# Attention scores of a two-layer macaron block in two float32r parts: maxima and weights on the two halves of TensorE's array

## The chip, the cores and the metric

The kernel runs on one core of a Trainium2 chip. The metric is the device time of one execution in microseconds. Before the change the median of three runs is 1638.24 us (1638.05 to 1641.87). Engines are written as the profile writes them: PE is TensorE's matmuls, PEld its weight loads, DVE VectorE, ACT ScalarE, POOL GpSimd, SP the engine whose queue issues most DMAs.

## What is computed

The input x has 16 batches of 512 tokens of width 128, in float32. Six sublayers follow each other, each on a layer norm of x and added to x:

```
x = x + 0.5 * kan(norm(x))        # per-feature two-layer perceptron on 64 features
x = x + attention(norm(x))        # 16 heads of width 8, 4 key heads, rotary, causal softmax
x = x + 0.5 * kan(norm(x))
x = x + 0.5 * experts(norm(x))    # 8 experts, each takes its 128 best tokens of a batch
x = x + recurrence(norm(x))       # gated linear recurrence over the tokens
x = x + 0.5 * experts(norm(x))
```

The change is in the attention:

```
q, k, v = x @ Wq, x @ Wk, x @ Wv              # 16, 4 and 4 heads of width 8; rotary on q and k
att = einsum('bhqd,bhkd->bhqk', q, k) / sqrt(8)
att = softmax(where(causal, att, lowest))
y = einsum('bhqk,bhkd->bhqd', att, v) @ Wo
```

The choice of the experts' tokens depends on everything before it, so the scores are computed to nearly float32 precision, out of products of low-precision parts.

## The kernel before

Every engine's order of instructions is written out by hand: generators emit work, and a loop calls them in turns. There are 44 turns per batch (`TURNS = NR * len(BANKS)`, 4 packs of 11 banks). In a turn the loop steps `weights(b)` and `maxima(b+1)` by one bank each, and then every generator in the lists `urgent` and `sides` by one step; what a step emits into `later` comes out at the start of the next turn. Side work asks `need` and `bank` for room: a turn has budgets of 1.5 us for PE, 1.15 for DVE, 0.85 for ACT and 1.45 for POOL, and a generator that finds too little waits for the next turn. An engine carries out its instructions in exactly the order in which the turns emitted them.

A batch goes through these steps:

- `kan` (first sublayer): norm, transposes (L319), two products of 512 columns (L339), eight activations (L372) with products into strips of 32 columns of the array, two groups of four (L366), and the output product (L387).
- `attn_in`: norm, products for queries (L425), rotated queries (L431), keys (L437, 512 columns on 64 columns of the array) and values (L445). VectorE multiplies by the rotary table (L426, L432, L438, L446), POOL adds. `parts` splits queries [128, 512] and keys [32, 512] into three bf16 parts: one copy on ACT (L397) and three steps on POOL (L400, L403, L406) each. `spread` writes the parts to DRAM, and DMAs on SP read them back into **packs**: `kp` with one batch's keys (3 buffers) and `qp` with four query heads of one key head r (10 buffers). A pack's 72 rows are the nine products of three parts by three parts, 8 dimensions each.
- `maxima(b+1)`: for each of four packs r and each of eleven banks, score products of queries by keys over the 72 rows into a PSUM bank `ps_sc` (L612, bf16, query tokens on the output's rows). A bank is one head of 512 or 384 keys, two heads of 256, or four of 128; banks of several heads first get a causal mask by a product with an identity (L608). VectorE then takes the row maxima (L617, L622). Two banks alternate.
- `max_rows`: for each half (two packs) VectorE negates the maxima and splits them into three bf16 parts (L632 to L638), TensorE transposes them (L643), and DMAs bring them by way of DRAM into rows 96 to 98 of the query packs. The key packs hold ones there, so that a product over 99 rows is a score less its row's maximum.
- `weights(b)`: the same scores transposed, keys on the output's rows, over 99 rows into `ps_st` (L675), then the exponential on ACT into `pt` (L678) and the causal cut on POOL (L680). In the last batch every other bank is called `ps_sl`.
- `outputs(b, r)`: `pt` by the values, four heads into four strips of 32 columns, 512, 384, 256 and 128 tokens wide (L698, PSUM `ps_av`, one buffer), a copy on ACT (L703), four transposes (L711), and a division on VectorE (L715, L716).
- `stage_out`: output product (L731), the next `kan`, norm and router scores (L751).

So `maxima` of a batch runs beside `weights` of the batch ahead of it. In one turn TensorE has all matmuls of a bank of weights, then all of a bank of maxima, then side work. After the last batch the packs' memory is taken by the experts' weights and tokens: weights are loaded at the start of the last batch, into packs that it doesn't use. The experts' phase (`experts`, L967, L980, with its combine in float32r, L931) takes the rest of the time.

Of the kernel before, what the change touches and what calls it, by code (L numbers as in the profile page):

```python
# [8 lines left out]
F32 = mybir.dt.float32  # L9
# [8 lines left out]
P = 128  # L18
S = 512
# [10 lines left out]
NQP = 10  # L30
NKP = 3
MXR = 96
# [16 lines left out]
def tile_macaron(  # L49
# [51 lines left out]
    with ExitStack() as ph:  # L101
# [54 lines left out]
        nc.scalar.dma_start(out=gate_sb, in_=gate_in)  # L156
        rbias = cst.tile([P, 2, NV], F32, name="rbias")

        w2d = cst.tile([P, 2, NV, MH], F32, name="w2d")
        eye4 = cst.tile([P, MH], F32, name="eye4")  # L160
# [6 lines left out]
        KR = NR * HD  # L167
        wq = cst.tile([D, NH, HD], F32, name="wq")
        nc.sync.dma_start(out=wq, in_=wq_in.rearrange("k (h d) -> k h d", d=HD))
        wk = cst.tile([D, 2, NR, HD], F32, name="wk")  # L170
        nc.sync.dma_start(out=wk[:, 0, :, :], in_=wk_in.rearrange("k (h d) -> k h d", d=HD))
# [3 lines left out]
        nc.sync.dma_start(out=wo, in_=wo_in)  # L175
# [3 lines left out]
        for b in range(1, B):  # L179
            load(b)  # L180
        hh = HD // 2
        wqr = cst.tile([D, NH, HD], F32, name="wqr")
        identb = cst.tile([P, P], BF16, name="identb")
# [3 lines left out]

        QP = [qkp.tile([P, NG, S], BF16, name=f"qp{i}", tag=f"qp{i}") for i in range(NQP)]
        KP = [qkp.tile([P, NR, S], BF16, name=f"kp{i}", tag=f"kp{i}") for i in range(NKP)]
        ROWS = slice(0, MXR + 3)  # L190

        def packed(b):
            return [QP[(NR * b + r) % NQP] for r in range(NR)], KP[b % NKP]

# [199 lines left out]
        def parts(r, dst, copies, **work):  # L394

            yield from need(**work)
            copies(dst[:, 0, :], r)  # L397
            yield
            yield from need(pool=1.15)
            nc.gpsimd.tensor_tensor(dst[:, 1, :], r, dst[:, 0, :], ALU.subtract)  # L400
            yield
            yield from need(pool=1.15)
            nc.gpsimd.tensor_tensor(r, r, dst[:, 0, :], ALU.subtract)  # L403
            yield
            yield from need(pool=1.3)
            nc.gpsimd.tensor_tensor(dst[:, 2, :], r, dst[:, 1, :], ALU.subtract)  # L406
            yield

        def spread(part, heads, name):

            scr = tc.dram_tile([3, HD, heads, S], BF16, name=name)
            for i in range(3):
                nc.sync.dma_start(out=scr[i].rearrange("d h t -> h d t"), in_=part[:, i, :])
            return scr

        def attn_in(b, st):
            _, xT = yield from norm(x[b])
            ka = w1p.tile([KR, S], F32, name="rope_ka")
            kb = w1p.tile([KR, S], F32, name="rope_kb")
            ta = w1p.tile([P, S], F32, name="rope_a")  # L420
            tb = w1p.tile([P, S], F32, name="rope_b")
            qpart = w1p.tile([P, 3, S], BF16, name="qpart")
            kpart = w1p.tile([KR, 3, S], BF16, name="kpart")
# [12 lines left out]
            pk = yield from bank([2 * KR, S], F32, "ps_pk", 0.9)  # L436
            nc.tensor.matmul(pk, lhsT=wk.rearrange("k w h d -> k (w h d)"), rhs=xT, start=True, stop=True)  # L437
            later.append(lambda: nc.vector.tensor_mul(ka, pk[0:KR, :], rope[0:KR, 0, :]))  # L438
# [3 lines left out]
            take(dve=0.7)  # L442
            pv = yield from bank([P, NT, KR], F32, "ps_v", 0.9)
            for c in range(NT):
                nc.tensor.matmul(pv[:, c, :], lhsT=xT[:, bass.ts(c, P)], rhs=wv, start=True, stop=True)  # L445
            later.append(lambda: nc.vector.tensor_mul(kb, pk[KR : 2 * KR, :], rope[KR : 2 * KR, 1, :]))  # L446
            yield
            take(dve=0.7)
            freed()
            qp_steps = parts(ta, qpart, nc.scalar.copy, act=0.6)  # L450
# [3 lines left out]
            nc.gpsimd.memset(va[:, :, :, HD:32], 0.0)  # L454
            nc.gpsimd.memset(va[:, :, :, HD : HD + 1], 1.0)
            later.append(lambda: nc.vector.tensor_copy(va[:, :, :, 0:HD], pv.rearrange("p c (r d) -> p c r d", d=HD)))
            yield
            take(dve=0.3)
# [3 lines left out]
            def keys():  # L462
                yield from need(pool=1.25)
                nc.gpsimd.tensor_tensor(ka, ka, kb, ALU.add)
                yield
                yield
                yield
                yield from parts(ka, kpart, nc.scalar.copy, act=0.6)

            yield from together(qp_steps, keys())  # L470
            qp, kp = packed(b)

            ks = spread(kpart, NR, f"ks{b}")
            qs = spread(qpart, NH, f"qs{b}")
            N = 3 * HD
            for j in range(3):
                nc.sync.dma_start(
                    out=kp[j * N : (j + 1) * N, :, :],
                    in_=ks[j].rearrange("d r t -> d (r t)").unsqueeze(0).to_broadcast([3, HD, NR * S]),
                )  # L480
            for r in range(NR):
                while taken[0] < NR * b + r - NQP + 1:
                    yield
                src = qs[:, :, r * NG : (r + 1) * NG, :].rearrange("i d h t -> (i d) (h t)")
                nc.sync.dma_start(out=qp[r][0 : 3 * N, :, :],
                                  in_=src.unsqueeze(0).to_broadcast([3, N, NG * S]))
            yield

        def centered(ps, w):

            ps = ps[:, 0 : w.shape[1]]
            nc.tensor.matmul(ps, lhsT=center, rhs=w, start=True, stop=True)
            nc.vector.tensor_copy(w, ps)
# [6 lines left out]
        def cleared(pack):  # L500

            nc.vector.memset(pack[MXR - 32 : MXR, :, :], 0.0)

        def keys_cleared(i):

            cleared(KP[i])
            nc.vector.memset(KP[i][MXR : MXR + 3, :, :], 1.0)

        def prepare():
# [26 lines left out]
            centered(psc[:, 1, :], wk[:, 0, :, :].rearrange("k h d -> k (h d)"))  # L536
# [5 lines left out]
            nc.vector.tensor_copy(wk[:, 1, :, 0:hh], wk[:, 0, :, hh:HD])  # L542
            nc.vector.tensor_copy(wk[:, 1, :, hh:HD], wk[:, 0, :, 0:hh])
# [5 lines left out]
            make_identity(nc, identb)  # L549
            nc.gpsimd.memset(causal[:, 0 : S - P], 0.0)  # L550
            make_causal_mask(nc, own, NEG)
            for i in range(1, NR):
                cleared(QP[i])
                yield
            for _ in range(16):
                yield
            for i in range(NR, NQP):
                if i - NR < NKP - 1:
                    keys_cleared(i - NR + 1)
                yield  # L560
                yield
                cleared(QP[i])
                yield
                yield
# [33 lines left out]
        def maxima(b, st):  # L598
            qp, kp = packed(b)
            for half in range(2):  # L600
                maxs = w2p.tile([P, NT, NH // 2], F32, name="maxs")
                for r in (2 * half, 2 * half + 1):
                    for c, gs in BANKS:
                        n = (c + 1) * P
                        v = in_bank(scp.tile([P, S], F32, name="ps_sc"), gs)
                        alone = len(gs) == 1
                        if not alone:
                            nc.tensor.matmul(v[:, :, n - P : n], lhsT=identb,  # L608
                                             rhs=own.unsqueeze(1).to_broadcast([P, len(gs), P]),
                                             start=True, stop=False, skip_group_check=True)  # L610
# [642 lines left out]
```

## Time and profile before

| | |
|---|---|
| median of three runs | 1638.24 us |
| the profiled execution's own time | 1638.15 us |
| its span on the engines | 1636.4 us |
| mean clock that TensorE was granted | 0.979 of full |
| PE, DVE, ACT, POOL busy | 1527.1, 1173.9, 988.6, 977.5 us |
| up to the first exponential | 119.1 us |
| the 15 batches that have maxima beside weights | 119.1 to 910.2 us |
| last batch | 910.2 to about 960 us |
| experts, recurrence, experts | about 960 to 1636.4 us |

How to read it: the span is from the first to the last instruction on the engines; the own time has what lies around it too. A group's line gives source line, engine, operation, written and read tile, shapes, count, then busy time and mean length of one instruction in ns. An fp32 matmul has two records (two passes), a bf16 or float32r matmul one. `72*128` stands for rows and columns of the array that a matmul uses: 128*32 is a strip of 32 columns, 64*128 half of the rows. A matmul's record includes the way through the array, so that records overlap; the distance from start to start is what the engine spends.

### The profile page before, as it was taken

The page shows a single profiled execution, that of the slowest core. Times are in us where ns is not written, and L with a number is a line of the kernel's source. Part 1 is how long each engine was busy: PE and PEld are TensorE (multiplying, and loading weights), DVE is VectorE, ACT ScalarE, POOL GpSimd, SP SyncE. Part 2 cuts the span into 40 slices and gives each one's busy share as a digit, 9 for nine tenths or more (in the row PEclk, how much of TensorE's full clock was granted, in tenths as well). Part 3 has the DMA queues.
Part 4 walks back from the last instruction along what each step waited for, and adds up shares of the span by engine and source line. Part 5 has one row for each costly group of instructions (what it writes and reads, how often), then busy time and mean ns, then how long its engine had stood idle before and what let it go on. Part 6 is the DMA issues. An engine that isn't in the chain of part 4 may idle for free.

```text
span 1636.4 us, 33218 instructions
## 1 busy us (share of the span) xinstructions
PE 1527.1 (93%) x11881; PEld 1062.5 (65%) x11881; DVE 1173.9 (72%) x3646; ACT 988.6 (60%) x1884; POOL 977.5 (60%) x1455
## 2 busy tenths in 40 slices
PE   5689999999999999999998899999998999999998
PEld 2234444454445444445444479999997999999998
DVE  6578878888888888888898345975579755873343
ACT  3336677877778777777766865444443444444443
POOL 2634566566655664665564666667665566756673
PEclk9779999999999999999999999999999999999999
DMA  5110110111011100110122113223322223323332
GB/s 128 64 69 24 55 54 26 42 55 53 32 40 52 57 25 36 57 47 29 42 71 69 51 44 69 59 54 72 72 68 56 66 62 72 78 51 74 67 67 58
DMA packets 99290, 92.74 MB, mean 57 GB/s; under 512 B 13245, under 2 KB 87686, under 8 KB 98886
## 3 DMA queue, kind: packets, MB, share of 16 engines
q1 hardware_dynamic: 76732, 67.72, 13.4%
q0 software_dynamic: 21584, 22.89, 7.7%
q8 instruction: 93, 1.52, 0.4%
q14 instruction: 71, 0.58, 0.1%
q10 hardware_dynamic: 810, 0.02, 0.0%
HBM read 59.07 MB, written 35.45 MB: 58 GB/s over the span
## 4 chain that ended last, share of the span: by engine, by line
PE 70%; DVE 20%; ACT 4%; issue 3%; POOL 2%; DMA 1%; SPq 0%; DVEq 0%; POOLq 0%; ACTq 0%
PE ps_h L967 12%; PE ps_y L980 12%; PE ps_av L698 7%; PE ps_st L675 6%; PE ps_sc L612 6%; DVE below L617 5%; PE acc L931 4%; PE ps_kg L366 3%; PE ps_s L339 3%; PE ps_t L319 3%; DVE ln_st L288 2%; ACT pt L678 2%; PE ps_ko L387 2%; DVE wk L801 2%; DVE tok L799 1%
## 5 line engine op out<-in xcount | busy, mean ns | idle before, releaser
L680 POOL TENSOR_SCALAR_AFFINE_SELECT pt<-pt 128x128 f32<-128x128 f32 (+2 forms) x704 | 253.2, 367 | 326.3 <-ACT pt L678 321.2
L678 ACT ACTIVATE pt<-ps_st 128x512 f32<-128x512 f32 x682 | 368.0, 563 | 94.5 <-PE ps_st L675 89.0
L617 DVE CUSTOM_DVE_ANT_0 below<-ps_sc,causal 128x512 bf16<-128x512 f32 (+1 forms) x512 | 315.2, 616 | 79.8 <-PE ps_sc L612 64.5
L870 POOL DMA_INDIRECT xg<-xnd,tokI x256 | 254.4, 994 | 86.7 <-issue 38.3
L969 ACT ACTIVATE mo<-ps_h 128x512 f32<-128x512 f32 x256 | 152.8, 597 | 228.1 <-PE ps_h L967 227.2
L967 PE MATMUL ps_h<-xin,mw 128*128 128x128 f32 x2048 | 273.8, 277 | 0.0
L980 PE MATMUL ps_y<-mw,mo 128*128 128x128 f32 x2048 | 272.0, 276 | 0.0
L612 PE MATMUL ps_sc<-kp,qp 72*128 72x512 bf16 (+3 forms) x1024 | 258.9, 304 | 12.6 <-DVE maxs L617 7.6
L675 PE MATMUL ps_st<-qp,kp 99*128 99x512 bf16 x992 | 249.9, 303 | 16.7 <-ACT pt L678 16.2
L967 PEld LDWEIGHTS ps_h<-xin,mw 128*128 128x128 f32 x2048 | 251.8, 193 | 12.8 <-issue 10.8
L980 PEld LDWEIGHTS ps_y<-mw,mo 128*128 128x128 f32 x2048 | 250.8, 193 | 0.1
L675 PEld LDWEIGHTS <-kp 99*128 99x128 bf16 x1024 | 94.4, 100 | 175.9 <-issue 158.4
L372 ACT ACTIVATE kan_h<-kan_s,rbias,kw 128x512 f32<-128x512 f32 x256 | 205.6, 812 | 4.1 <-PE ps_kg L366 4.1
L997 POOL DMA_INDIRECT sum<-mo,tokI x93 | 151.4, 1628 | 75.7 <-ACT mo L969 16.6
L698 PE MATMUL ps_av<-pt,va 128*32 128x512 f32 (+3 forms) x2048 | 165.2, 440 | 0.0
L622 DVE TENSOR_REDUCE maxs<-ps_sc 128x2 f32<-128x512 f32 (+1 forms) x192 | 130.1, 685 | 35.0 <-PE ps_sc L612 34.5
L612 PEld LDWEIGHTS <-qp 72*128 72x128 bf16 x1024 | 96.0, 99 | 80.4 <-issue 58.0
L698 PEld LDWEIGHTS ps_av<-pt,va 128*32 128x32 f32 x2048 | 53.5, 109 | 93.6 <-issue 42.5
L295 POOL TENSOR_TENSOR ln_rstd<-ln_rstd,mhalf 128x4 f32<-128x4 f32 x96 | 102.7, 1069 | 8.0
L294 POOL TENSOR_SCALAR ln_rstd<-ln_mv 128x4 f32<-128x4 f32 x96 | 22.0, 229 | 119.6 <-DVE ln_mv L292 119.4
L319 PE MATMUL ps_t<-ident,kan_x 128*128 128x128 f32 x384 | 63.5, 289 | 30.8 <-DVE kan_x L309 21.4
L986 DVE SCALAR_TENSOR_TENSOR ye<-ps_y,gainT,ye 128x128 fp32r<-128x128 f32 x83 | 28.8, 347 | 83.4 <-ACT ye L983 83.1
(196 smaller groups left out, 2487.5 us busy)
## 6 DMA issues: line engine op xcount, KB each, us to landing
qp<-qs SPq DMA_DIRECT2D x64, 288.0 KB
xnd<-kan_x SPq DMA_DIRECT2D x32, 256.0 KB
sum<-x SPq DMA_DIRECT2D x62, 128.0 KB
qs<-qpart SPq DMA_DIRECT2D x48, 128.0 KB
kp<-ks SPq DMA_DIRECT2D x48, 96.0 KB
x<-in_L_attn_x_dram SPq DMA_DIRECT2D x16, 256.0 KB
mw<-in_L_ffn_w_dram SPq DMA_DIRECT2D x16, 256.0 KB
xg<-xnd,tokI POOLq DMA_INDIRECT x256, 2.6
```

The lines of the kernel that those rows point to most:

```text
L372: nc.scalar.activation(h, sk[half], AF.Relu, bias=rbias[:, half, v : v + 1], scale=kw1[:, half, v : v + 1])
L612: nc.tensor.matmul(v[:, u, 0:n], lhsT=qp[r][0 : 9 * HD, g, bass.ts(c, P)], rhs=kp[0 : 9 * HD, r, 0:n], start=alone, stop=(u == len(gs) - 1 ...
L617: nc.vector.tensor_tensor_reduce(below[:, 0:n], v[:, 0, 0:n], causal[:, S - n : S], 1.0, LOWEST, ALU.add, ALU.max, accum_out=maxs[:, c, h ...
L675: nc.tensor.matmul(v[:, u, 0:n], lhsT=kp[ROWS, r, bass.ts(c, P)], rhs=qp[r][ROWS, g, c * P : S], start=True, stop=True)
L678: nc.scalar.activation(o, v[:, :, 0:n], AF.Exp, scale=HD ** -0.5)
L680: nc.gpsimd.affine_select(out=dg, in_=dg, compare_op=ALU.is_ge, fill=0.0, base=0, pattern=[[0, len(gs)], [1, P]], channel_multiplier=-1)
L698: nc.tensor.matmul(po[32 * g : 32 * g + 32, c * P : S], lhsT=va[:, c, r, :], rhs=pt[:, g, OFF[c] : OFF[c] + n], start=(c == 0), stop=(c == ...
L870: nc.gpsimd.indirect_dma_start(out=xgs[i // E % 2][:, i % E, :], out_offset=None, in_=xnd[b], in_offset=bass.IndirectOffsetOnAxis(ap=tokI[ ...
L967: nc.tensor.matmul(pst[:, f, :], lhsT=mw1[e][:, bass.ts(f, P)], rhs=xins[i // E % 2][:, i % E, :], start=True, stop=True)
L969: nc.scalar.activation(hs[u], pst, AF.Gelu)
L980: nc.tensor.matmul(py, lhsT=hs[u][:, f, :], rhs=mw2[e][:, f, :], start=(f == 0), stop=(f == NF - 1))
L997: nc.gpsimd.indirect_dma_start(out=sums[k, b], out_offset=bass.IndirectOffsetOnAxis(ap=tokI[g][:, n : n + 1], axis=0), in_=added[b % 2 * ( ...
```

## The change

- Queries and keys are split into two float32r parts instead of three bf16 parts (float32r is float32 with a short mantissa, for TensorE). Scores are the four products of two parts by two parts, on 32 rows.
- A pack is float32 and has two halves. Rows 0 to 63 (32 products, 32 rows of zeros on the keys' side) serve `maxima`; rows 64 to 97 (32 products, two rows for the maximum's two parts) serve `weights`. A query pack thus holds a later batch in its upper half and an earlier one in its lower. There are 4 query packs and 2 key packs; each half is loaded again when the products that read it are emitted (`feed`, `put_keys`, `put_queries`).
- `weights` and `maxima` no longer emit their matmuls. They yield them, and `both` emits them alternately, one of weights, one of maxima, so that neighbours stand on different halves of the array's rows. The reading operations of both banks come behind.
- The mask of a bank of maxima is two products on 64 rows (two halves of an identity) instead of one on 128.
- The maxima go to one fp32 tile per half (`topped`), are transposed by one fp32 transpose, and are split into two parts behind it by two operations on 32 rows.
- Keys are computed as four blocks of tokens in four strips of 32 columns, twice (plain and rotated), so that the rotary product, the sum and the parts are [128, 128] instead of [32, 512].
- `outputs` accumulates two packs r into one `ps_av` (values of odd packs stand 16 columns further), so there are half as many copies and divisions and two groups of transposes per batch instead of four. The rows of Wo are loaded in a matching order, in eight DMAs.
- In the last batch the experts' weights are loaded as packs come free, and the gathered tokens use the first and last query pack.

The core of the diff:

```diff
-        QP = [qkp.tile([P, NG, S], BF16, name=f"qp{i}", tag=f"qp{i}") for i in range(NQP)]
-        KP = [qkp.tile([P, NR, S], BF16, name=f"kp{i}", tag=f"kp{i}") for i in range(NKP)]
-        ROWS = slice(0, MXR + 3)
+        QP = [qkp.tile([P, NG, S], F32, name=f"qp{i}", tag=f"qp{i}") for i in range(NR)]
+        KP = [qkp.tile([P, NR, S], F32, name=f"kp{i}", tag=f"kp{i}") for i in range(NKP)]
+        UP, LOW = slice(0, KM), slice(KM, ONE + 2)
...
+            while ready("km", 1, maxed, NR * NKP - NR + 1):
+                put_keys("km", 0)
+            while ready("qm", NR, maxed, NR):
+                put_queries("qm", 0)
+            while ready("kw", 1, taken, NR * NKP - NR + 1):
+                put_keys("kw", KM)
+            while ready("qw", NR, taken, NR):
+                put_queries("qw", KM)
...
                         if not alone:
-                            nc.tensor.matmul(v[:, :, n - P : n], lhsT=identb,
-                                             rhs=own.unsqueeze(1).to_broadcast([P, len(gs), P]),
-                                             start=True, stop=False, skip_group_check=True)
+                            for i in range(2):
+                                runs.append((v[:, :, n - P : n], eyes[:, i, :],
+                                             owns[:, i, :].unsqueeze(1).to_broadcast([KM, len(gs), P]), i == 0, False))
                         for u, g in enumerate(gs):
-                            nc.tensor.matmul(v[:, u, 0:n], lhsT=qp[r][0 : 9 * HD, g, bass.ts(c, P)],
-                                             rhs=kp[0 : 9 * HD, r, 0:n],
-                                             start=alone, stop=(u == len(gs) - 1), skip_group_check=True)
+                            runs.append((v[:, u, 0:n], qp[UP, g, bass.ts(c, P)], kp[UP, r, 0:n],
+                                         alone, u == len(gs) - 1))
...
-            nc.vector.tensor_scalar_mul(ms[:, :, 0, :], maxs, -1.0)
-            nc.vector.scalar_tensor_tensor(r, in0=maxs, scalar=-1.0, in1=ms[:, :, 0, :],
-                                           op0=ALU.mult, op1=ALU.subtract)
...
+            nc.tensor.transpose(pm, topped[half], ident)
+            r = pm[0:N, :]
+            mr = w1p.tile([N, 2, P], F32R, name="mr")
...
-                    for u, g in enumerate(gs):
-                        nc.tensor.matmul(v[:, u, 0:n], lhsT=kp[ROWS, r, bass.ts(c, P)],
-                                         rhs=qp[r][ROWS, g, c * P : S], start=True, stop=True)
+                    runs = [(v[:, u, 0:n], kp[LOW, r, bass.ts(c, P)], qp[LOW, g, c * P : S], True, True)
+                            for u, g in enumerate(gs)]
...
+        def both(*gs):
+
+            got = [g for g in (next(g, None) for g in gs if g is not None) if g is not None]
+            for i in range(max((len(runs) for runs, _ in got), default=0)):
+                for runs, _ in got:
+                    for out_, w, m, start, stop in runs[i : i + 1]:
+                        nc.tensor.matmul(out_, lhsT=w, rhs=m, start=start, stop=stop, skip_group_check=True)
+            for _, read in got:
+                read()
...
-                step(wts)
-                step(mxs)
+                both(wts, mxs)
```

## The prediction

> **What bounds the kernel now.** I read the page first, then a table of the busy time by stretches, then the chain of work inside one stretch, then the order of TensorE's matmuls there. Section 1 and the chain's shares:
>
> ```profile
> PE 1527.1 (93%) x11881; PEld 1062.5 (65%) x11881; DVE 1173.9 (72%) x3646; ACT 988.6 (60%) x1884; POOL 977.5 (60%) x1455
> ...
> PE 70%; DVE 20%; ACT 4%; issue 3%; POOL 2%; DMA 1%; SPq 0%; DVEq 0%; POOLq 0%; ACTq 0%
> ```
>
> TensorE leads, but the change touches only the attention, so its stage decides. The first exponential of each of the 16 batches starts at 119.1, 162.9, 212.6, 267.7 us and so on to 910.2: one period per batch. Three of them by engine (length, then PE, PEld, DVE, ACT, POOL busy, clock, DMA share):
>
> ```profile
> 162.90:212.60 49.70, 45.75 (x348) 22.37 (x347) 40.11 (x127) 34.10 (x64) 32.06 (x65) 1.00 0.17 55
> ...
> 483.40:537.30 53.90, 51.57 (x401) 26.23 (x399) 45.44 (x143) 42.31 (x78) 33.12 (x64) 1.00 0.14 45
> ...
> 862.40:910.20 47.80, 43.67 (x360) 22.58 (x353) 38.15 (x130) 33.43 (x65) 18.77 (x49) 1.00 0.20 64
> ```
>
> A middle period takes 53.9 us. The chain inside it is 37.0 us TensorE, 12.6 us VectorE, 4.3 us the rest. VectorE's part is two stretches; this is the first:
>
> ```profile
> 484.41 1.22 DVE ms_r L633
> 485.63 0.03 issue
> 485.67 0.68 DVE rope_kb L446
> 486.35 0.03 issue
> 486.38 0.69 DVE below L617
> ```
>
> So there are two bounds: TensorE in most turns, VectorE where normalization, rotation and maxima meet. DMA is far from a bound (share 0.14).
>
> **What a score matmul costs, and what surrounds it.** The order of matmuls at the start of that period (start, length, of which the tail is modelled; starts are what counts):
>
> ```profile
> 482.89 0.39 PE L675 MATMUL ps_st<-qp,kp 99*128 99x512 bf16 x1
> 483.12 0.38 PE L612 MATMUL ps_sc<-kp,qp 72*128 72x512 bf16 x1
> 483.34 0.97 PE L445 MATMUL ps_v<-wv,kan_xT 128*128 128x32 f32 x8
> 484.15 0.38 PE L675 MATMUL ps_st<-qp,kp 99*128 99x512 bf16 x1
> 484.37 0.38 PE L612 MATMUL ps_sc<-kp,qp 72*128 72x512 bf16 x1
> 484.68 1.06 PE L698 MATMUL ps_av<-pt,va 128*32 128x512 f32 x8
> 485.68 0.39 PE L675 MATMUL ps_st<-qp,kp 99*128 99x512 bf16 x1
> ```
>
> Three prices stand here. A bf16 score of 512 columns takes 0.22 us (482.89 to 483.12 to 483.34), and going on to another full-array matmul costs nothing. Four products into 32-column strips run side by side: the eight records of L698 take 1.00 us, where one fp32 product of 512 columns alone takes 0.86. And a change of the array's division costs time: 484.37 + 0.22 = 484.59, but L698 starts at 484.68, so about 0.10 us to change; the same on the way back.
>
> The changed scores stand on 64 rows each. The trace has 64-row matmuls in one place:
>
> ```profile
> 1454.19 1.06 PE L980 MATMUL ps_y<-mw,mo 128*128 128x128 f32 x8
> 1455.17 0.28 PE L814 MATMUL ps_r<-ident,tokf 64*128 64x64 f32 x1
> 1455.29 0.22 PE L815 MATMUL ps_r<-ident,gain 64*128 64x64 f32 x1
> 1455.44 0.94 PE L967 MATMUL ps_h<-xin,mw 128*128 128x128 f32 x6
> ```
>
> Eight passes at 0.111 end at 1455.08 and L814 starts 0.09 later; on the way back it is again 0.10. Behind a change the first 4-byte weights are also not loaded ahead: the eight records of L967 after such a change run 1049.71 to 1050.71, 1.00 us, where eight of the same shape without a change (L731, 498.88 to 499.77) take 0.89: 0.10 us more. A bf16 score after a change shows none of that (485.68 to 485.90 is 0.22). Float32r is priced by the combine: ten products of 256 columns in 1.19 us on the chain, 0.119 each, about 0.01 over the bf16 price; its weight loads have the mean of fp32's (193 ns both, against 99 for bf16), so I give it fp32's 0.107 per load (0.111 per pass in L967 is its ceiling).
>
> **The change part by part, per middle period (four packs r).**
>
> Scores. Before, a pack costs, from 0.22, 0.165, 0.11 and 0.055 us for 512, 384, 256 and 128 columns: banks of 512, 4 × 0.44; of 384, 4 × 0.33; of 256 with mask, 2 × 0.55; the last, 4 + 4 matmuls of 128 and a mask of 512, 0.66. After, if the halves work side by side as strips do, a bank costs its longer half: 4 × 0.23; 4 × 0.17; two masks and two products, 2 × 0.46; and 2 × 0.22 of masks plus four 128-column products held at 0.107 by their loads, 0.86. Gains 0.84, 0.64, 0.18 and −0.20: 1.46 a pack, **5.8 us a period**.
>
> Changes of division. Counted in the two programs' order: before, 30 changes a period, all to or from strips, and none between scores and full-array work. After, 18 entries into the scores from full-array work and 19 exits to it, at 0.10 + 0.10 each: 37 × 0.2 = 7.4; 12 entries from strips, each now with an exposed load, 1.2; strips next to full work 0.4; fewer strip changes −0.4. **+8.6 us.**
>
> Other TensorE work. Two of four groups of oT transposes go (0.44 each, 0.9); maxima as one fp32 transpose instead of four bf16, −0.2; keys as two strip groups instead of 512 columns on 64 strips, −0.3. Sum for TensorE: −5.8 + 8.6 − 1.4 = **+1.4 us a period**. That is the heart: the pairing is paid back at the borders.
>
> VectorE, means by shape over 16 batches. Out: five operations on the maxima (13.7 + 13.0 + 13.0 + 8.2 + 7.3 = 55.2 us, 3.45 a period), two rotated-key products (1.36), reciprocals and divisions (2.13). In: two 32-row operations per half at about 0.29 and 0.35 (L531, L986), 1.3; one 256-column product, 0.42 (L940); divisions of pairs, 1.35; values +0.1. −3.8 of 45.4. POOL: the third bf16 part goes (L403, L406: 74.3 us, 4.6 a period), the key steps shrink from 32x512 to 128x128 (39.0 us, 2.4, to 0.7): −6.3. ACT: two oT copies (1.17) and a shorter key copy: −1.4. None of POOL's and ACT's is on the chain of a middle period. VectorE's is: of the first stretch ms_r 1.22, both key rotations 1.36 and ms 0.2 go, with 0.95 of waiting between ms and its transpose; 1.1 comes back. That is up to 2.6; TensorE has its own work below, so I take 2.3. A middle period: 53.9 + 1.4 − 2.3 = 53.0, and eleven of them: **−10 us**. The four light periods (two first, two last) have only 12 to 22 borders to full-array work, so TensorE's sum falls by 2 to 4 there; it is not always the bound, half is −6. Together **−16 us**.
>
> Rows no longer shown bound the unseen: a pair of 512 columns lies between 0.22 (full overlap) and 0.44 (none); I take 0.23, nearest to the strips' row. A load behind a change lies between 0.00 (bf16's row) and 0.10 (fp32's); I take 0.10, by the equal record length.
>
> DMA. A period moves 64-row float32 packs: eight writes of 256 KB and four of 128 KB, plus parts of twice the size, about 1.3 MB more in 53.9 us, 24 GB/s beside 45. Each pack is refilled once read and used 33 turns later (some 40 us); a qp refill takes SP 0.75 us. Hidden; without that cover each late pack would cost its landing, a few us a period.
>
> Start, −6 us. On the chain before 80 us stand VectorE's clears of packs (about 7 us from 32.5 to 42) and POOL's part steps twice (45.5 to 53.8, 66.2 to 73.3); I count 12 of these some 22 us as gone, as other engines are near. Against it POOL clears the second key pack (2048 columns, twice; at 0.42 us for 384, about 4.4 us), and unpaired maxima with 21 borders cost TensorE some 4; I let 2 of these 8 be hidden. End, +2: in the last period weights are unpaired, 21 borders, TensorE +5 of 49.8, of which its 20 us share on the chain lets less than half through. Expert weights now load as packs come free, a period's quarter ahead of use.
>
> Sum: 1636.4 − 16 − 6 + 2 = 1616.4; what lies around the span is 1638.15 − 1636.4 = 1.75: **1618 us**. The profiled execution is 0.1 under the median 1638.24.
>
> [...]
>
> **Rivals.**
> - **The two halves' weight loads take turns** (slower). The strips' four loads start 7 ns apart, which speaks against it; but they share the columns, not the rows. The second load then adds 0.107 at some 30 entries a period (3.2 us, less where masks lead) and holds the 128-column products: +3 us a period with TensorE leading, 13 periods: 1618 + 39 = 1657. It decides from 0.04 us per entry on.
> - **The halves do not overlap.** The pairs' 2.3 us a pack come back, 9 us in each of 15 periods: about 1755. For it: nothing; against: strips.
> - **Float32r loads as cheaply as bf16.** Borders shrink by half, TensorE −4 us a period; VectorE's 41.6 of busy time then holds the period near 50: about 1574. Against it: 193 ns.
>
> **How the numbers follow.** Forecast's case 0.54: spread ±20 around 1618, so 0.40 faster, 0.06 same, 0.08 slower. Loads in turn 0.25: 0.01 same, 0.24 slower. No overlap 0.08: slower. Cheap loads 0.13: faster. Faster by over 0.3% 0.53, within 0.3% 0.07, slower 0.40; 0.3% is about what a measurement of this kernel can tell from no change. Range 1570 to 1690: it holds cheap loads and loads in turn, and leaves out no overlap and what lies beyond.
>
> **What would show it.** Pairs: starts of ps_st and ps_sc of one bank within some 10 ns, the next 0.23 later. Borders: 0.10 of gap and 0.10 more on the first matmul behind. DVE busy near 41.6 and POOL near 27 in a middle period. It would be wrong if ps_sc started 0.1 or 0.2 behind ps_st, if the bank of 128 columns took over 1 us, or if a ps_st waited for a DMA.

## The result and the profile after

The changed kernel takes 1737.13 us (median of 4 runs, 1731.67 to 1740.8), the kernel before 1640.05 beside it. The ratio is 1.0598, 95% interval 1.0571 to 1.0625: **slower by 6%**, outside the range given. The profiled execution took 1740.61 us, with a span of 1738.9 against 1636.4, 102.5 us more. By the first exponential of each batch, 8.3 us of that come ahead of batch 0 (127.4 against 119.1), 79.0 between batch 0 and batch 15 (870.1 against 791.1), and 15.2 behind. Ratios compare fast runs; of all runs below one is a slow one (over 1.5% above its kernel's fastest), the profiled run of experiment 2, and it is left out of that experiment's times.

The page of the kernel after: TensorE's, and all engines', busy time, the granted TensorE clock in 40 slices (tenths), and the engines' shares of the chain.

```profile
PE 1643.8 (95%) x12073; PEld 1135.4 (65%) x12073; DVE 1113.5 (64%) x3472; ACT 968.7 (56%) x1852; POOL 893.3 (51%) x1415
...
PEclk9757878799999999898978779999999999999999
...
PE 78%; DVE 13%; ACT 5%; POOL 2%; issue 1%; DMA 1%; SPq 0%; ACTq 0%; DVEq 0%
```

The clock line of the kernel before:

```profile
PEclk9779999999999999999999999999999999999999
```

This is the line that the prediction passed over. Behind the start the kernel before has 0.9 or more in every slice; the changed one is below that in 13 of the first 24, up to the end of the attention, and at 0.5 in one. Over the span the granted clock is 0.912, and was 0.979.

The stretches that answer to those of the prediction (length, then PE, PEld, DVE, ACT and POOL busy, clock, DMA share, GB/s): a light period, two middle ones, the last.

```profile
180.70:236.50 55.80, 52.23 (x361) 26.82 (x360) 38.16 (x118) 33.15 (x63) 25.23 (x59) 0.84 0.30 77
...
367.00:420.20 53.20, 52.51 (x414) 28.33 (x410) 40.80 (x133) 40.52 (x77) 27.65 (x62) 1.00 0.28 69
...
474.90:529.50 54.60, 53.90 (x414) 28.42 (x410) 40.71 (x133) 40.42 (x77) 27.56 (x63) 0.97 0.27 68
...
934.40:997.50 63.10, 59.28 (x356) 28.99 (x355) 36.73 (x116) 32.98 (x62) 19.02 (x50) 0.72 0.15 38
```

The one middle period at full clock takes 53.2 us, where 53.0 was forecast: the working of that period held. Its neighbours carry the same 414 matmuls in 54.6, with one half-clock window (below) in each, so that such a window costs 1.4 us there. The last period, with fewer matmuls, takes 63.1 at a clock of 0.72.

The trace records the clock as full or half, in windows of 3.41 us: each of the 104 clock records of before and after reads 1.0 or 0.5, and each but the last of a trace lasts a multiple of 3.413 us. Here is one half window and what lies around it, in a middle period:

```profile
452.40:455.80 3.40, 3.40 (x29) 2.64 (x28) 2.64 (x8) 2.56 (x5) 0.73 (x3) 1.00 0.00 0
455.80:459.20 3.40, 3.25 (x24) 1.77 (x22) 3.30 (x13) 3.40 (x7) 3.05 (x6) 1.00 0.25 72
459.20:462.60 3.40, 3.40 (x22) 0.91 (x18) 2.28 (x6) 1.94 (x4) 2.27 (x5) 0.50 0.34 92
462.60:466.00 3.40, 3.40 (x40) 1.63 (x32) 2.07 (x10) 2.06 (x5) 0.85 (x4) 1.00 0.00 0
```

TensorE is busy for 3.25 of 3.40 us in the second row, and the third gets half the clock. What differs is what the matmuls use of the array. I call **use** the sum, over the matmul records of a window, of rows/128 × columns/128 × streaming time at full clock (in the traces about 0.22 us for 512 columns of bf16, 0.226 in the median of 492 score products of before, and 0.43 for 512 columns in one record of fp32, 0.432 in L339; for float32r 0.22 is an estimate: where two pairs of 512 columns follow each other in after, the second starts 0.335 us behind the first, in the median of 13, and 0.11 of that is the load), as a share of the window. The four rows have a use of 0.60, 0.34, 0.46 and 0.70. "A use below 0.37 is followed by half a clock, another by the full one" was fitted on the first traces; in the trace of before it is wrong for 8 of 478 windows, in that of after for 10 of 507. The share of the window in which anything streams, whatever its rows and columns, does as well for before (5 wrong at its best bound) but not for after (31). Before, 27 windows are at half clock, 19 of them ahead of 120 us; after, 94, with 22 ahead of 120 us. These counts take the time ahead of a trace's first clock record (25.1 us before, 18.9 after) as half clock; in the records themselves there are 20 and 90. In full-clock windows between 375 and 580 us the mean use falls from 0.69 to 0.59. The scores account for it: with 2.2 us of streaming a pack, 8.8 a period, they use an estimated 8.8 × (72 + 99)/128 of 53.9 us before, 0.22, and 8.8 × (64 + 34)/128 of 53.2 after, 0.13. The same columns stream on fewer rows, and the borders take most of the time that the pairing frees (53.2 us a middle period at full clock, 53.9 before).

### The profile page after: what moved, and what is told of

It is laid out like the page before. It is cut to its first block, busy times and chain, and to the rows that moved or that the text cites. A ratio compares the mean times of both kernels' runs of the same rounds, so it can differ in the third digit from the quotient of the medians.

```text
span 1738.9 us, 33538 instructions
## 1 busy us (share of the span) xinstructions
PE 1643.8 (95%) x12073; PEld 1135.4 (65%) x12073; DVE 1113.5 (64%) x3472; ACT 968.7 (56%) x1852; POOL 893.3 (51%) x1415
## 4 chain that ended last, share of the span: by engine, by line
PE 78%; DVE 13%; ACT 5%; POOL 2%; issue 1%; DMA 1%; SPq 0%; ACTq 0%; DVEq 0%
PE ps_h L1032 11%; PE ps_y L1045 11%; PE ps_st L734 11%; PE ps_av L753 10%; PE ps_sc L734 6%; PE acc L996 4%; PE ps_s L348 4%; PE ps_kg L375 4%; PE ps_t L328 3%; ACT pt L719 3%; PE ps_ko L396 2%; DVE below L653 2%; PE ps_g L814 2%; DVE wk L864 1%; DVE tok L862 1%; DVE ln_st L297 1%
## 5 line engine op out<-in xcount | busy, mean ns | idle before, releaser
L734 PE MATMUL ps_sc<-kp,qp 64*128 64x512 f32 (+3 forms) x1024 | 367.7, 427 | 9.2 <-DVE topped L653 7.4
L734 PE MATMUL ps_st<-qp,kp 34*128 34x512 f32 x992 | 338.2, 411 | 22.0 <-ACT pt L719 19.8
L734 PEld LDWEIGHTS ps_st<-qp,kp 34*128 34x128 f32 x992 | 170.6, 202 | 274.6 <-ACT pt L719 157.4
L1032 PE MATMUL ps_h<-xin,mw 128*128 128x128 f32 x2048 | 273.8, 277 | 0.0
L1032 PEld LDWEIGHTS ps_h<-xin,mw 128*128 128x128 f32 x2048 | 251.8, 193 | 13.0 <-issue 10.8
L734 PEld LDWEIGHTS ps_sc<-kp,qp 64*128 64x128 f32 x1024 | 188.1, 211 | 39.8 <-DVE topped L653 16.6
L753 PE MATMUL ps_av<-pt,va 128*32 128x512 f32 (+3 forms) x2048 | 196.1, 506 | 0.0
L658 DVE TENSOR_REDUCE topped<-ps_sc 128x2 f32<-128x512 f32 (+1 forms) x192 | 130.3, 684 | 37.6 <-PE ps_sc L734 36.7
L734 PE MATMUL ps_sc<-owns,eyes 64*128 64x256 bf16 (+1 forms) x384 | 97.9, 338 | 7.5 <-DVE topped L653 6.5
L375 PE MATMUL ps_kg<-kan_h,w2d 128*32 128x512 f32 x512 | 92.0, 718 | 3.4 <-ACT kan_h L381 3.4
```

What stands on the lines that cost most here:

```text
L375: nc.tensor.matmul(pg[o : o + MH, :], lhsT=w2d[:, half, v, :], rhs=h, start=(t < U), stop=(t == U))
L734: nc.tensor.matmul(out_, lhsT=w, rhs=m, start=start, stop=stop, skip_group_check=True)
L753: nc.tensor.matmul(po[32 * g : 32 * g + 32, c * P : S], lhsT=va[:, c, r, :], rhs=pt[:, g, OFF[c] : OFF[c] + n], start=(c == 0 and not odd) ...
L1032: nc.tensor.matmul(pst[:, f, :], lhsT=mw1[e][:, bass.ts(f, P)], rhs=xins[i // E % 2][:, i % E, :], start=True, stop=True)
```

## The experiments

**Theory A**: the change's own costs are about as forecast, and the loss is the clock, which follows the use of the array. Rivals: B, the clock follows something else in the change (float32r, the changes of division); C, it follows how long TensorE streams, not rows; and that float32r or the borders cost more than forecast.

### 1. Scores on the whole array, unpaired

```diff
-        UP, LOW = slice(0, KM), slice(KM, ONE + 2)
+        KQ = qkp.tile([P, NR, S], F32, name="kq", tag="kq")
+        UP, LOW = slice(0, ONE), slice(0, ONE + 2)
...
-            kp = KP[b % NKP][:, :, :].bitcast(F32R)
+            kp = KQ[:, :, :].bitcast(F32R)
```

The maxima's keys have a tile of their own, loaded pack by pack; other rows of both key tiles are zeros, and the mask is one product of 128 rows again.

> The change without its pairing: scores still as four float32r products with all else of the change, but maxima read 96 rows and weights 98 rows of the packs, with zeros in the keys where the other half's rows stand, so every score matmul is on the whole array and there are no borders between scores and full-array work. Theory (the clock): what made the change slow is that half-array scores let the granted clock fall; here it returns to about 0.97 of full over the run and a middle period takes 53 to 54 us, 1615 to 1645 us in all. Rival (the rest of the change costs the time: float32r, refills of packs, the later start): the clock stays near 0.91 and the time over 1700 us.

Measured: 1694.81 us (1688.52 to 1697.86), ratio 1.0329 [1.0296, 1.0361]; clock 0.966, 38 half-clock windows. The clock came back, and the mean use with it (0.69), but the time only in part: that half of the expectation failed. Middle periods at clock 1.00 take 55.0 us, so unpaired float32r scores cost 1.8 a period more than the pairs with their borders (53.2).

### 2. and 3. More use: zero rows, and useless partners

```diff
-        UP, LOW = slice(0, KM), slice(KM, ONE + 2)
+        UP, LOW = slice(0, KM), slice(KM, P)
```

The 30 rows added to the weights' products are zeros.

> The changed kernel with weights on 64 rows instead of 34 (30 rows of zeros added on both sides); order, columns, borders and overlap are as before. Theory (the clock follows the share of the array that matmuls use, rows counted as used): the share of a pair rises from 98 to 128 rows, the clock from 0.91 to 0.93 or more, 15 to 50 us less. Rival (only the time counts in which something streams, or the rows are counted by halves): no change, within 8 us of 1737.

Measured: 1718.23 us (median of three, 1702.5 to 1721.25), ratio 1.0456 [1.0398, 1.0514], clocks 0.927 to 0.941. The profiled execution took 1728.89 us; its clock is 0.924, with 82 half-clock windows. So zeros on idle rows make the kernel some 19 us faster.

```diff
+            if gs[0] is None and got and got[0][0]:
+                ps = stp.tile([P, S], F32, name="ps_st")
+                got.insert(0, None)
+                got[0] = ([(ps[:, 0 : m.free_size()], some[KM:P, 0:P], some[KM:P, 0 : m.free_size()], True, True)
+                           for _, _, m, _, _ in got[1][0]], lambda: None)
```

Ahead of batch 0 the maxima stand alone on one half; here a useless bf16 product runs beside each on the other half.

> The changed kernel with a partner for the lone maxima of the first batch (ahead of the first exponential): a bf16 product of the same columns on the array's other half, into a free bank that nobody reads. It adds work that lies beside other work. Theory (share of the array): the clock between 80 us and the first exponential rises from 0.57 to over 0.8, and the first exponential comes 8 to 20 us earlier than at 127 us. Rival (streaming time): the clock there stays within 0.05 of 0.57 and the first exponential within 4 us.

Measured: 1732.44 us (1729.94 to 1738.65), ratio 1.0579 [1.0548, 1.061]. The same 40 us, in the kernel after and in this one:

```profile
80.00:120.00 40.00, 37.23 (x119) 18.44 (x119) 24.27 (x71) 8.56 (x13) 6.55 (x10) 0.59 0.14 38
```

```profile
80.00:120.00 40.00, 33.85 (x209) 16.32 (x209) 25.80 (x75) 11.15 (x17) 6.54 (x10) 0.87 0.14 38
```

90 matmuls more, and TensorE is busy for less time, for the clock rises from 0.59 to 0.87. From the first matmul of the maxima to the first exponential it takes 53.8 us instead of 60.9, and the first exponential comes at 120.1 instead of 127.4. That the whole kernel gains is not shown: the median is 5 us lower, but the intervals of the two ratios overlap.

### 4. Useless products in the narrow banks

```diff
+                        if (c, gs) in BANKS[9:]:
+                            runs.append((ps, some[0:KM, 0:P], some[0:KM, :], True, True))
...
+                    if i >= 9:
+                        runs.insert(0, (ps, some[KM:P, 0:P], some[KM:P, :], True, True))
```

> The changed kernel with one useless bf16 product of 512 columns ahead of the real ones in each of the last two banks of a pack, on both halves (written to the bank and then overwritten by the real products): 128 pairs by 0.22 us are 28 us of added TensorE work. Theory A: the granted clock of a 3.41 us window follows the use of the array in the window before, use being the sum over matmuls of rows/128 x columns/128 x streaming time at full clock; in the traces so far a window with a use below about 0.37 is followed by half a clock. The low windows of the changed kernel lie at exactly these narrow banks. Laid on its trace, the added work leaves 68 half-clock windows of 94; each costs 1.7 us, so 44 us come back and 28 go: about 15 us less than the changed kernel (1715 to 1730), clock 0.93 to 0.94. Theory B: the clock follows something else of the change (the float32r products themselves, or the number of changes of the array's division): the added work changes neither, so the clock stays at 0.91 and the time rises by 25 to 30 us (1760 to 1770).

Measured: 1730.7 us (1728.49 to 1732.63), ratio 1.0554 [1.054, 1.0567]; clock 0.935, 73 half-clock windows. Theory B (1760 and more) is out: work was added, and the time fell by 6 us. Five middle periods in a row look like this:

```profile
477.70:532.00 54.30, 53.66 (x430) 29.52 (x426) 40.80 (x133) 40.78 (x77) 27.61 (x63) 1.00 0.27 67
```

The half-clock window is gone and the period is 0.3 us shorter than the 54.6 without the added work. The gain in the whole is at the lower edge of what was expected.

### 5. Fewer rows, the same instructions

```diff
-                            runs.append((v[:, u, 0:n], qp[UP, g, bass.ts(c, P)], kp[UP, r, 0:n],
+                            runs.append((v[:, u, 0:n], qp[0:34, g, bass.ts(c, P)], kp[0:34, r, 0:n],
```

> The changed kernel with the maxima's products on 34 rows instead of 64; the 30 rows left out hold zeros in the keys, so the result is the same, and every instruction, its columns and its half of the array stay. Theory A (use counts rows): half-clock windows rise from 94 to about 108, clock 0.89 to 0.90, 15 to 30 us more than the changed kernel (1750 to 1770). Theory C (the clock follows how long TensorE streams, whatever the rows): no change, 1732 to 1742, clock 0.91.

Measured: **1781.38 us** (1772.39 to 1793.32), ratio 1.0878 [1.0835, 1.0921]; clock 0.887, 122 half-clock windows. A middle period and the last one:

```profile
491.80:547.90 56.10, 55.39 (x414) 28.91 (x410) 40.69 (x133) 40.42 (x76) 27.56 (x62) 0.94 0.26 66
...
970.30:1037.80 67.50, 64.17 (x355) 32.18 (x355) 36.93 (x116) 33.25 (x62) 19.05 (x50) 0.65 0.15 37
```

The middle period ahead of the first one shown has the full clock:

```profile
438.60:491.80 53.20, 52.50 (x414) 28.34 (x410) 40.76 (x133) 40.49 (x77) 27.62 (x63) 1.00 0.29 70
```

Not one instruction more or less, 30 rows of zeros left out, and 44 us are lost. At full clock the period takes 53.2 us here as in the kernel after, so the products themselves cost the same, and the loss comes with the clock. This is the cleanest test here: C is out, and rows count, zeros or not. It went further than expected (122 windows where 108 were worked out).

### 6. The first experiment on 128 rows

```diff
-        UP, LOW = slice(0, ONE), slice(0, ONE + 2)
+        UP, LOW = slice(0, P), slice(0, P)
```

> The kernel of the first experiment (float32r scores on the whole array, nothing paired) with its products on 128 rows instead of 96 and 98; the rows added hold zeros. No instruction is added in the loops. Theory A: half-clock windows fall from 38 to about 23, clock 0.966 to about 0.98, 15 to 25 us less than that kernel (1670 to 1682). Theory C: no change (1690 to 1698). In both, it stays slower than the kernel before: at full clock the unpaired float32r products themselves cost about 35 us (1694.8 less 57.6 lost to the clock, against 1636.4 less 34.4).

Measured: 1678.67 us (1676.29 to 1683.97), ratio 1.0244 [1.0225, 1.0262]; clock 0.976, 29 half-clock windows. As expected by A, and 16 us under experiment 1, by zeros alone. Since this kernel keeps the full clock nearly throughout, it shows a second thing. Three of its periods:

```profile
220.20:281.20 61.00, 55.77 (x401) 34.90 (x400) 45.37 (x146) 40.24 (x75) 24.71 (x57) 1.00 0.26 61
...
451.20:505.90 54.70, 53.24 (x402) 33.70 (x398) 40.91 (x133) 40.89 (x77) 27.00 (x63) 1.00 0.27 68
...
726.60:788.20 61.60, 59.15 (x436) 35.85 (x434) 48.19 (x153) 42.38 (x78) 28.95 (x65) 1.00 0.26 66
```

In the kernel before, the period in the place of the last one is

```profile
702.90:758.60 55.70, 53.39 (x400) 27.08 (x400) 48.65 (x160) 42.00 (x78) 32.13 (x64) 1.00 0.13 43
```

61.0, 60.5 (281.2 to 341.7) and 61.6 us stand where before has 55.1, 53.9 and 55.7: 18.4 us that owe hardly anything to the clock. In the last of them a batch's key and value products have slipped a period: 48 instead of 24, none in the period ahead. The kernel after has the same slip, and the same three long periods (66.8, 63.7, 64.2).

### 7. All that raises the use

The edits of 2, 3 and 4 together.

> The changed kernel with all that raises the use: weights on 64 rows (30 of them zeros), useless partners beside the lone maxima ahead of batch 0, and the useless products in the last two banks of each pack. Theory A: on the trace of the variant with 64 rows the added products leave 46 half-clock windows of 82, and the partners take some 8 more: clock about 0.955 to 0.965, and 1719.7 less 5, less 61, plus 28: 1670 to 1690. Theory B: the clock stays near 0.92 and the time goes to 1735 to 1750. It would beat the kernel before only with hardly a half-clock window left.

Measured: 1708.44 us (1703.01 to 1712.12), ratio 1.0415 [1.0394, 1.0436]; clock 0.957, 50 half-clock windows. The clock is as expected, the time 18 us over. The expectation put nearly 1.7 us on each window saved. The 44 windows saved against the kernel after, at the 0.9 to 1.5 us that variants with other rows give (see below), are an estimated 40 to 66 us; 16 batches of added products at 1.1 (54.3 less 53.2 in experiment 4) to 1.8 (as worked out) take back 18 to 29. That leaves 11 to 48, and 29 were measured.

### 8. to 10. Another order of the banks

```diff
+        BANKS = [BANKS[i] for i in (0, 8, 1, 4, 5, 10, 6, 7, 2, 9, 3)]
...
-                    if c == NT - 1:
+                    if i == len(BANKS) - 1:
                         taken[0] = NR * b + r + 1
```

The narrow banks, where many low windows lie, are spread among the wide ones: in the kernel after, in the kernel after with the edits of 2 and 3, and in the kernel before as a control.

> The changed kernel with the eleven banks of a pack in another order, the three narrow ones (two of 256 columns, one of 128) spread among the wide ones instead of together at the end; the same instructions, nothing added. Theory A (the use within one window of 3.41 us decides, and the low windows are those that hold the narrow banks together): fewer half-clock windows, 40 to 65 instead of 94, clock 0.935 to 0.955, 1665 to 1700. Theory E (the mean use over a longer stretch decides, or the number of products): the order changes nothing, clock 0.91, 1730 to 1745.

> The same order, with the weights' products on 64 rows (30 of them zeros) and the useless partners beside the lone maxima ahead of batch 0. Theory A: the rows raise every window that holds pairs, the partners the stretch ahead of batch 0: clock 0.955 to 0.97, 1640 to 1670; it would beat the kernel before only at the clock of that kernel, 0.98. Theory E: as the variants with 64 rows and with partners alone, 1715 to 1735.

> Control: the kernel before with its banks in that order. It has hardly a window below 0.37 behind 120 us of the span, so by theory A there is nothing to win: clock 0.975 to 0.98, 1632 to 1648. If the order alone is worth something (to VectorE, ScalarE or the pacing of the side work), it shows here without the clock.

Measured: 1769.37 us (ratio 1.081 [1.0778, 1.0842]; clock 0.908, 100 half-clock windows), 1736.95 (1.0609 [1.0577, 1.064]; clock 0.931, 78) and 1657.98 (1.0117 [1.0098, 1.0136]; clock 0.975, 31). All three expectations failed. In the control the order alone costs 19 us (a middle period at full clock takes 54.6 us instead of 53.9), so it is worse for other reasons; which, stays open. And it doesn't lift the low windows: the mean use in full-clock windows from 375 to 580 us falls from 0.594 to 0.572, and the new low windows hold wide pairs with their borders and few full-array products. So the narrow banks alone are not what makes a window low. What its low windows lack is side work: by the matmul records from 320 to 870 us, strips and full-array products use 0.5 us of the full array in a full-clock window below 0.37 and 1.5 in the others; in the kernel after it is 0.4 and 1.5. The bound of 0.37 is wrong here for 18 of 515 windows, its worst but one.

### 11. and 12. The rule carried to the kernel before

```diff
-                            nc.tensor.matmul(v[:, u, 0:n], lhsT=qp[r][0 : 9 * HD, g, bass.ts(c, P)],
-                                             rhs=kp[0 : 9 * HD, r, 0:n],
+                            nc.tensor.matmul(v[:, u, 0:n], lhsT=qp[r][0:MXR, g, bass.ts(c, P)],
+                                             rhs=kp[0:MXR, r, 0:n],
```

and for 12 also:

```diff
+                        if b == 0:
+                            nc.tensor.matmul(ps, lhsT=identb, rhs=causal, start=True, stop=True, skip_group_check=True)
```

> The kernel before with the maxima's bf16 products on 96 rows instead of 72; the 24 rows added hold zeros that are there already, so no instruction is added anywhere. Theory A (the clock follows the use, in whatever kernel): its half-clock windows, 19 of 27 ahead of 120 us where the lone maxima of batch 0 run, fall by about 4; 3 to 8 us less than the kernel before. Theory C (rows do not count): no change.

> The same, with one useless bf16 product of 512 columns on the whole array ahead of each of the 44 banks of batch 0's maxima (overwritten by the real products): 9.4 us of added TensorE work at full clock, in the stretch from 76 to 119 us of the span, where the granted clock is about 0.6. Theory A: nearly no half-clock window is left in that stretch, the first exponential comes 5 to 10 us earlier, and the time is 6 to 14 us less than the kernel before (1625 to 1633). Theory C or B: the clock stays, and the added work makes it 5 to 10 us longer.

Measured: 1637.91 us against 1638.22, ratio 0.9998 [0.9986, 1.0009], and 1635.73, ratio 0.9986 [0.9975, 0.9998]. The stretch ahead of batch 0 in the kernel before, and in number 12:

```profile
76.00:119.00 43.00, 35.32 (x138) 15.72 (x139) 35.60 (x106) 14.49 (x22) 14.84 (x16) 0.74 0.20 72
```

```profile
76.00:119.00 43.00, 39.01 (x190) 16.99 (x187) 36.06 (x108) 16.33 (x27) 15.42 (x18) 0.95 0.20 70
```

In number 12 the clock does what A says (0.74 to 0.95), but the time missed A's range: from the first matmul of the maxima to the first exponential it takes 50.2 us instead of 51.0, and 2.5 us are left in the whole, less than 0.3%. VectorE is busy for 36 of these 43 us and may hold the stretch as well; that was not tested. Number 11 is the same as the kernel before, where A expected 3 to 8 us less and 4 half-clock windows fewer (worked out from the runs' clocks, the median has 20 instead of 22). So by itself it cannot tell A from C; experiments 2, 5 and 6 do. Number 12 is faster by less than 0.3%; a version of the changed kernel that beats the kernel before was not found.

## Why the prediction was wrong

- **The step that failed** is the sum itself: "A middle period: 53.9 + 1.4 − 2.3 = 53.0, and eleven of them". It prices the new matmuls at full clock, takes for granted that the clock of before stays, and no rival speaks of the clock. In its place the clock fell from 0.979 to 0.912, with 94 half-clock windows instead of 27. By its terms: start −6 became +8.3, the eleven middle periods −10 became +40.6, the four light ones −6 became +38.4, and the end +2 became +15.2, together 102.5 us. The clock column stood in the lines shown (1.00), and the page shows 0.7 in the slices before 120 us, where the kernel before has lone maxima on 72 rows: the warning was there.
- **What the clock costs.** 94 half-clock windows against 27 are 67 more; one can cost at most an estimated 1.7 us, half of 3.41, as a product takes twice as long at half clock (0.43 against 0.22 us for 512 columns of bf16, before). Where a middle period has one of them it costs 1.4 (54.6 against 53.2). Between kernels that differ in zero rows alone, the medians of span and of windows (for each run 2 × (1 − clock) × span / 3.41) give 44.3 us for 30 windows (5 and after), 18.9 for 20 (after and 2) and 16.1 for 13 (1 and 6): 1.5, 0.9 and 1.2 each. 67 windows at 0.9 to 1.5 are an estimated 60 to 101 of the 102.5 us.
- **Pairs overlap: right.** The rows behind this, in the kernel after:

```profile
499.96 1.07 PE L753 MATMUL ps_av<-pt,va 128*32 128x512 f32 x8
500.96 0.49 PE L734 MATMUL ps_st<-qp,kp 34*128 34x512 f32 x1
500.96 0.49 PE L734 MATMUL ps_sc<-kp,qp 64*128 64x512 f32 x1
501.39 1.13 PE L348 MATMUL ps_s<-kan_xT,win 128*128 128x512 f32 x2
502.44 0.49 PE L734 MATMUL ps_st<-qp,kp 34*128 34x512 f32 x1
```

Both halves start at 500.96, and the next full-array matmul at 501.39: 0.43, which is 0.22 of streaming with 0.11 for the load (fp32 records of only 8 columns, L751 before, follow each other at 0.112 us) and 0.10 for the change of division. By itself 0.43 could also be two products in turn (0.44). Two pairs of 384 columns that follow each other decide it:

```profile
518.38 0.66 PE L328 MATMUL ps_t<-ident,kan_x 128*128 128x128 f32 x4
518.97 0.44 PE L734 MATMUL ps_st<-qp,kp 34*128 34x384 f32 x1
518.97 0.44 PE L734 MATMUL ps_sc<-kp,qp 64*128 64x384 f32 x1
519.25 0.34 PE L734 MATMUL ps_st<-qp,kp 34*128 34x384 f32 x1
519.25 0.34 PE L734 MATMUL ps_sc<-kp,qp 64*128 64x384 f32 x1
519.52 1.06 PE L375 MATMUL ps_kg<-kan_h,w2d 128*32 128x512 f32 x8
```

The first pair takes 0.28, which is 0.17 and one load; the second takes 0.27, which is 0.17 and the change to the strips, where two products in turn would stream for 0.33. The two loads of the first pair cost 0.11 together, and in the second pair none shows. So the rivals are out: loads in turn, no overlap, and loads as cheap as bf16's. The bank of 128 columns did take over 1 us, which the prediction had named as a sign of being wrong: 1.07 in the median of 35 banks between 320 and 870 us at full clock, up to the next matmul and with what it waits for, 0.39 more than before. Where the next pair follows at once it is 0.84, with 0.86 forecast.
- **Borders: right.** L348's two passes of 0.43 take 1.05 from 501.39 to 502.44, 0.1 for the weights behind the change and 0.1 for the change back.
- **VectorE and POOL: right.** 40.8 and 27.6 us busy in a middle period, where 41.6 and about 27 were forecast; TensorE 52.5 against 51.6 (+0.9, forecast +1.4). DMA stayed hidden: none stands on the chain between 127.4 and 997.5 us.
- **Start, −6: wrong, +8.3.** What was to go went: the first matmul of the maxima is 1.5 us earlier (66.6 against 68.1). But TensorE on half an array then ran 40 us at a clock of 0.59. With partners it is +1.0 (experiment 3), so up to 7 us were mis-sized besides the clock; which of the terms, stays open.
- **Light periods, −6: wrong, +38.4.** The four grew by 9.5, 6.1, 7.5 and 15.3 us, with 32 half-clock windows where before has 1: there the pairs have few full-array products between them. The last has grown most of all periods, 63.1 against 47.8 at a clock of 0.72.
- **End, +2: wrong, +15.2.** All of it lies in the last batch: from its first exponential to the experts' first product (L967, now L1032) it takes 57.6 us (997.5 to 1055.1) instead of 42.4 (910.2 to 952.6), and from there on both kernels take 683.8. In it 7 windows are at half clock, where before has none: at 0.9 to 1.5 an estimated 6 to 11 us. What the rest is stays open.
- **Three long periods**, 18.4 us in experiment 6 and nearly all of it at full clock, were not seen: the count of matmuls by period would have shown only the slip of key and value products, and what lengthens the other two stays open.
- **Open**: whether the changed kernel would be faster than before at that kernel's clock. 1738.9 less 60 to 101 is 1638 to 1679, at or above 1636.4; at the 1.7 that a window can cost at most it would be 1625. So a gain is not shown, and the measured prices speak against it.

## What to carry to other kernels

Here the same products on fewer rows, side by side, took 0.7 us off a middle period at full clock (53.2 us against 53.9), while the mean use of the array fell from 0.69 to 0.59 and the granted clock over the span from 0.979 to 0.912, and an estimated 60 to 101 of the 102.5 us lost went with the clock. For a change of this kind, add up rows × columns × time per window of 3.41 us before and after, and look at the clock line first. Rows of zeros on the products that stream anyway, without a new instruction in the loops, were worth 19 us here and 16 in another form, and 44 were lost where they were taken away; the kernel before gained nothing from them. Useless products paid little: 6 us in experiment 4, and 2.5 in number 12, where TensorE was not the only busy engine.

## What the runs showed of the hardware

- In these traces the clock stands in windows of 3.41 us, full or half (104 records in before and after, all 1.0 or 0.5). With the bound of 0.37 on the use of the window before, 5 to 20 of some 500 windows are wrong in each of the 14 traces. Rows that hold zeros count (44 us in experiment 5). That columns count like rows is part of the fit and was not tried by itself.
- Use counts streaming time at full clock, and at half clock a product streams for twice as long: a bf16 score of 512 columns takes 0.43 us in before at half clock and 0.22 at full, an fp32 record of 512 columns (L339) 0.85 and 0.43. By the fitted bound a window at half clock must therefore stream on an estimated 0.75 of the array (2 × 0.37) to get the clock back; lone scores on half an array fall short of that estimate. In the kernel after the clock stayed half from 90.6 to 145.2 us, with TensorE busy for 52.2 of these 54.6 us.
- A busy TensorE did not keep the clock: in the kernel after the window at 455.8 was busy for 3.25 of 3.40 us, with a use of 0.34, and the next ran at half clock.
- Going from scores to strips or to full-array products, and back, took about 0.10 us each way: in before L698 starts at 484.68 behind a score that streams to 484.59, and in after 0.27 us for a pair of 384 columns ahead of strips, where 0.17 is streaming. The first 4-byte weights behind such a change took 0.1 us more (eight records of 128 columns in 1.00 us behind one and in 0.89 without, in before).
